# A Mamba block with attention and FFN on one core: six products on GpSimd instead of four, and their rows of C loaded in the last unit

## The chip, the cores and the metric

The kernel runs on one core of a Trainium2 chip. The metric is the device time of one execution in microseconds, from the first to the last instruction of the program with what lies around it; the lower, the better.

## What is computed

The input x is (8, 96, 64, 64): 8 batches, 96 channels, 4096 positions. Layer 0 is a group norm, a Mamba block (selective scan) and a residual. Layer 1 is linear attention and an FFN with rounding to an 8-bit float, each with a layer norm and a residual. The change concerns the selective scan alone, which runs over L = 4096 positions for 192 inner channels and 16 states:

```
dA  = exp(delta[..., None] * A)
dBu = delta[..., None] * Bm[:, :, None, :] * u[..., None]
h   = dA_t * h + dBu_t                     # for each position t
y_t = einsum('ben,bn->be', h, C_t)         # sum over the 16 states
y   = y + u * D
y   = y * silu(z);  out = y @ out_proj_w.T;  layernorm(out)
```

## The kernel before

The eight batches are taken as four pairs p. A pair's 4096 positions are cut into 8 chunks c of T = 512, so there are 32 chunks. The state of a scan is carried from chunk to chunk.

In a chunk the scan has 24 **units** u. `where(u)` (L555) gives j = u // 8 (three blocks of 64 inner channels), g = (u // 2) % 4 (four groups of four states) and b = u % 2 (half of the channels); a unit is 128 partitions (4 states x 32 channels) by 2 batches by 512 positions. The work of one unit, in the order in which `unit` (L611) issues it:

- `pooled` (L667): if the unit before is in POOLED, its product pr = hs * C is issued here on GpSimd, with C from an SBUF tile `c`.
- `rows_c` (L566): for the next unit, unless that is in POOLED, a matmul on TensorE (L571) spreads the rows of C over the partitions into a PSUM tile `cc` (two buffers).
- `sums` (L588): on even units, matmuls on TensorE (L595) add the products of two units, over their states, into the PSUM tile `y`. For pooled units the call stands elsewhere (L656 before the change).
- waiting norm work on GpSimd, then part 0 of the unit's steps.
- `products_b` (L558): dbu = du * B on GpSimd, three units ahead (AHEAD = 3, four buffers).
- the scans (L639): two instructions on VectorE, which need the decay `da` in PSUM (two buffers); behind each, `decay` (L575) issues the exponential of the next unit on ScalarE (L581).
- in each eighth unit `gate` (L607) on VectorE multiplies y with silu(z), and `skip` (L600) opens the next y.
- part 1 of the steps, and last, unless the unit is pooled, the product pr = hs * cc on VectorE (L663).

`hs`, a scan's output, has three buffers; a pooled product (`pq`) has two, another product four.

All other work is cut into pieces, by generators, and a table STEPS, written by hand, says which pieces are issued in which unit and part. P is the projection of the chunk after the next (convolution L450, SiLU L483 and L484, x_proj L489, its copies L494 and L497, dt_proj L507, delta L511). E is the output of the chunk before (projection L691, its copy L699, gains L718, transposes L707 with the additions L741 and L746, Gram products L759). F0 and F1 are the attention and FFN of an older chunk, from chunk 9 on (transposes L831, copy L834, L838, transposes L854, rounding L857, first layer L864 with L871, second layer L903, copy L908, end L915). G is the group norm of the next pair.

SILU = 10 is a unit after which ScalarE loads another table and runs the SiLU; the decays of unit 12 are issued ahead of it, into two other PSUM banks.

Before the change POOLED is (2, 3, 10, 11) and POOLED_G = 1: the units of group 1 for j = 0 and j = 1. The tile `c` has one buffer. `rows` (L541) fills it for the next chunk by four DMAs of 128 KB, issued by SP in unit 17, where group 1 of j = 0 and 1 has been used. [...]

Of the kernel before, what the change touches and what calls it, by code (L numbers as in the profile page):

```python
# [19 lines left out]
NU = NJ * NG * 2  # L20
# [1 line left out]
NK = T // 128  # L22
HID = 384
RANK = 6
POOLED = (2, 3, 10, 11)
POOLED_G = 1
SILU = 10
ROWS_B = (16, 18, 20, 22)
AHEAD = 3
# [36 lines left out]
def tile_mamba_linear_attention_ffn(  # L66
# [62 lines left out]
    def rsqrt(out_, var, eps):  # L129

        nc.gpsimd.tensor_scalar_add(out_, var, eps)
        nc.gpsimd.tensor_tensor(  # L132
            out_, out_, mhalf[0 : out_.shape[0], 0 : out_.shape[1]], op=ALU.pow
        )
# [245 lines left out]
    def later(kind, work):  # L380
        if kind in waiting:
            waiting[kind].append(work)
        else:
            work()

    def now(kind):
        for work in waiting[kind]:
            work()
        waiting[kind].clear()

    def norm_stats(src, n, tag):

        mv = p2.tile([128, n, 2], F32, tag=f"mv{tag}", name="mv")
        rstd = p2.tile([128, n], F32, tag=f"rs{tag}", name="rs")
        nmr = p2.tile([128, n], F32, tag=f"nm{tag}", name="nm")
        st = p2.tile([128, n, 6], F32, tag=f"st{tag}", name="st")
        for i in range(n):
            nc.vector.bn_stats(st[:, i, :], src[:, i, :])  # L398
        for i in range(n):
            nc.vector.bn_aggr(mv[:, i, :], st[:, i, :])  # L400

        def ends():
            nc.gpsimd.tensor_scalar_mul(nmr, mv[:, :, 0], -1.0)  # L403
            rsqrt(rstd, mv[:, :, 1], 1e-5)
            nc.gpsimd.tensor_mul(nmr, nmr, rstd)

        later("norms", ends)
        return rstd, nmr
# [132 lines left out]
    def rows(s, to, of, g):  # L541

        t = s[to, g] = p2.tile([128, 2, T], F32, tag=to, name=to, bufs=NG if to == "b" else 1)
        for n in range(NG):
            nc.sync.dma_start(
                t[32 * n : 32 * n + 32],
                s["bd"][of : of + 2 * NS].rearrange("(b n) t -> n b t", b=2)[NG * g + n]
                .unsqueeze(0)
                .to_broadcast([32, 2, T]),
            )  # L550

    def rows_b(s, g):
        rows(s, "b", 0, g)

    def where(u):  # L555
        return u // (2 * NG), (u // 2) % NG, u % 2

    def products_b(s, u):  # L558
        j, g, b = where(u)
        dbu = s["dbu", u] = p2.tile([128, 2, T], F32, tag="dbu", name="dbu", bufs=AHEAD + 1)  # L560
        nc.gpsimd.tensor_mul(  # L561
            dbu, s["du", j][:, 2 * b : 2 * b + 2, :],
            s["b", g][:, b, :].unsqueeze(1).to_broadcast([128, 2, T]),
        )

    def rows_c(s, u):  # L566
        j, g, b = where(u)
        if u in POOLED:
            return
        cc = s["cc", u] = ps_all.tile([128, T], F32, tag="cc", name="cc", bufs=2)  # L570
        nc.tensor.matmul(  # L571
            cc, lhsT=sel[64:128, g, b], rhs=s["cs"][64:128, :], start=True, stop=True
        )

    def decay(s, u, h, bank=None):  # L575
        if ("da", u, h) in s:
            return
        j, g, b = where(u)
        da = psum(bank) if bank else ps_all.tile([128, T], F32, tag="da", name="da", bufs=2)
        s["da", u, h] = da  # L580
        nc.scalar.activation(  # L581
            da, s["dl", j][:, 2 * b + h, :], AF.Exp, scale=aneg[:, 2 * j + h, g : g + 1]
        )
# [4 lines left out]
    def sums(s, u):  # L588

        j, g, _ = where(u)  # L590
        for b in range(2):
            pr = s.pop(("pr", u - 1 + b))
            for h in range(2):
                q = 64 * b + 32 * h
                nc.tensor.matmul(  # L595
                    s["y"][q : q + 32, :], lhsT=ssum, rhs=pr[:, h, :],
                    start=False, stop=(g == NG - 1),
                )

    def skip(s, j):  # L600

        s["y"] = ps_all.tile([128, T], F32, tag="y", name="y", bufs=1)
        nc.tensor.matmul(  # L603
            s["y"], lhsT=dd[:, j, :], rhs=s["xm"][:, j, :], start=True, stop=False
        )

    def gate(s, j):  # L607
        zs = s["zs"][:, j, :]
        nc.vector.tensor_mul(zs, s["y"], zs)  # L609

    def unit(s, prev, nxt, first, u, steps):  # L611
        def at(v):
            return (s, v) if v < NU else (nxt, v - NU)


        if u - 1 in POOLED:
            pooled(s, u - 1)
        if u:
            nc.scalar.copy(state["new"][:, u - 1, :], s.pop(("hs", u - 1))[:, :, T - 1])  # L619
        else:  # L620
            if prev is not None:
                nc.scalar.copy(state["new"][:, NU - 1, :], prev.pop(("hs", NU - 1))[:, :, T - 1])
            state["last"] = state.get("new")
            state["new"] = p2.tile([128, NU, 2], F32, tag="state", name="state")
        to, v = at(u + 1)
        if to is not None:
            rows_c(to, v)
        if u % 2 == 0 and (u or prev is not None) and (u - 1) not in POOLED:
            sums(s if u else prev, (u or NU) - 1)
        now("norms")  # L630
        steps(u, 0)
        to, v = at(u + AHEAD)
        if to is not None:
            products_b(to, v)
        hs = s["hs", u] = p2.tile([128, 2, T], F32, tag="hs", name="hs", bufs=3)
        dbu = s.pop(("dbu", u))
        to, v = at(u + 1)
        for h in range(2):
            nc.vector.tensor_tensor_scan(  # L639
                hs[:, h, :], s.pop(("da", u, h)), dbu[:, h, :],  # L640
                0.0 if first else state["last"][:, u, h : h + 1], ALU.mult, ALU.add,
            )
            if to is not None:
                decay(to, v, h)
        now("others")

        new = u % (2 * NG) == 1
        if new and u > 1:
            gate(s, u // (2 * NG) - 1)
        elif new and prev is not None:  # L650
            gate(prev, NJ - 1)
        if u == SILU and (nxt is not None):
            for h in range(2):
                decay(s, u + 2, h, ("mp", "mE")[h])
        steps(u, 1)
        if u - 4 in POOLED and u % 2:  # L656
            sums(s, u - 4)
        if new:
            skip(s, u // (2 * NG))
        if u in POOLED:  # L660
            return
        pr = s["pr", u] = p2.tile([128, 2, T], F32, tag="pr", name="pr", bufs=4)
        nc.vector.tensor_mul(  # L663
            pr, hs, s.pop(("cc", u)).unsqueeze(1).to_broadcast([128, 2, T])
        )

    def pooled(s, u):  # L667
        j, g, b = where(u)
        pr = s["pr", u] = p2.tile([128, 2, T], F32, tag="pq", name="pr")
        nc.gpsimd.tensor_mul(  # L670
            pr, s["hs", u], s["c", g][:, b, :].unsqueeze(1).to_broadcast([128, 2, T])
        )
# [5 lines left out]
    def chain_e(p, c, s):  # L678
# [51 lines left out]
        projected(1, ps)  # L730
        yield
        norm = norm_stats(o, 2 * NK, "o")
        yield
        for part in range(4):
# [197 lines left out]
    for g in range(NG):  # L932
        rows_b(slots[0], g)
    rows(slots[0], "c", 2 * NS, POOLED_G)
    spread(slots[0], 0)
# [46 lines left out]
    with tc.manual_schedule():  # L982
        for u in range(AHEAD):
            products_b(slots[0], u)
        for h in range(2):
            decay(slots[0], 0, h)
        rows_c(slots[0], 0)
        for i, (p, c) in enumerate(chunks):
            s = slots[i]
            prev = slots[i - 1] if i else None  # L990
            nxt = slots[i + 1] if i + 1 < N else None

            def steps(u, part):
                if part == 0:
                    if u in (0, 2 * NG):
                        spread(s, 1 + u // (2 * NG))
                    if nxt is not None and u == 18:
                        spread(nxt, 0)
                    if nxt is not None and u in ROWS_B:
                        rows_b(nxt, ROWS_B.index(u))  # L1000
                    if nxt is not None and u == 17:
                        rows(nxt, "c", 2 * NS, POOLED_G)
                for name in (STEPS[u] + "|").split("|")[part].split():
                    step(name, i, u)

            for u in range(NU):
                unit(s, prev, nxt, c == 0, u, steps)
# [4 lines left out]
    s = slots[N - 1]  # L1012
# [69 lines left out]
```

## Time and profile before

| | |
|---|---|
| median of 3 runs | 3535.59 us (3532.91 to 3539.99) |
| profiled execution | 3550.77 us, span 3549.1 us |
| TensorE (PE) busy | 2708.4 us, 76% |
| VectorE (DVE) busy | 3017.3 us, 85% |
| ScalarE (ACT) busy | 2277.4 us, 64% |
| GpSimd (POOL) busy | 2689.0 us, 76% |
| mean granted TensorE clock | 0.730 |
| DMA, mean | 125 GB/s |

Busy shares are means over all stages. A line of the groups gives line, engine, operation, output <- inputs, shapes and count, then busy us and the mean ns of one, then the idle time of the engine just before these instructions and what ended it. A line of the waits reads: engine and line that waited <- what ended the wait: us in total, times, longest us. A line of the timeline gives start, length, engine, line, operation and tiles, and in brackets the idle time before it. A matmul in 32-bit floats stands as two instructions in the counts.

### The profile page before, as it was taken

To read this page: it belongs to the slowest core of one execution; us is meant where nothing else is said; L and a number is where in the kernel's file an instruction comes from. 1 tells how busy PE (TensorE), PEld (TensorE's weight loads), DVE (VectorE), ACT (ScalarE), POOL (GpSimd) and SP (SyncE) were. 2 spreads that over 40 slices of the span, in tenths; PEclk is the share of its full clock that TensorE was granted. 3 is DMA by queue.
4 is the path that set the end of the run, shared out by engine and by line. 5 is a ranking of instruction groups with operands and counts; after the bars stand their busy time and mean duration, and the time that the engine had idled before them with its cause. 6 is when DMAs were issued, how large, how long until landed. Compare 5 with 4: busy or idle time off the path is not lost.

```text
span 3549.1 us, 35756 instructions
## 1 busy us (share of the span) xinstructions
PE 2708.4 (76%) x9770; PEld 1011.7 (29%) x9770; DVE 3017.3 (85%) x4345; ACT 2277.4 (64%) x4347; POOL 2689.0 (76%) x1838
## 2 busy tenths in 40 slices
PE   5577777778787777877878877777788787887677
PEld 1122222222223222322223322222233232332244
DVE  2699999899998889888889888899888888988934
ACT  2456666566666666666666666666776766676556
POOL 1778888788878787778777778778877878777734
PEclk8667777677766787776787677778866777775667
DMA  2555555555554456554456554455544445545212
GB/s 80 127 128 139 134 141 142 143 131 133 136 149 107 104 139 154 138 129 108 112 139 154 131 138 105 117 134 150 149 124 121 99 121 144 152 119 139 72 59 61
DMA packets 252399, 444.05 MB, mean 125 GB/s; under 512 B 36965, under 2 KB 53542, under 8 KB 252198
## 3 DMA queue, kind: packets, MB, share of 16 engines
q1 hardware_dynamic: 248982, 441.70, 49.2%
q8 instruction: 77, 1.26, 0.2%
q14 instruction: 124, 1.02, 0.1%
q10 hardware_dynamic: 3216, 0.07, 0.1%
HBM read 349.24 MB, written 92.41 MB: 124 GB/s over the span
## 4 chain that ended last, share of the span: by engine, by line
DVE 39%; PE 25%; ACT 12%; issue 9%; POOL 7%; DMA 2%; SPq 1%; DVEq 0%; POOLq 0%; ACTq 0%
DVE hs L639 25%; PE mp L450 7%; DVE pr L663 7%; PE y L595 4%; POOL dbu L561 3%; DVE st L398 3%; ACT da L581 2%; PE cc L571 2%; PE mE L759 2%; PE mp L507 1%; PE mp L489 1%; PE mE L691 1%; POOL pr L670 1%; DVE mv L400 1%; DMA b<-bd 1%
## 5 line engine op out<-in xcount | busy, mean ns | idle before, releaser
L561 POOL TENSOR_TENSOR dbu<-du,b 128x1024 f32<-128x1024 f32 x768 | 1802.9, 2362 | 220.2 <-DVE hs L639 106.7
L639 DVE TENSOR_TENSOR_SCAN hs<-da,state,dbu 128x512 f32<-128x512 f32 x1290 | 1575.7, 1267 | 260.3 <-ACT da L581 252.2
L581 ACT ACTIVATE da<-dl,aneg 128x512 f32<-128x512 f32 x1474 | 999.1, 688 | 780.9 <-DVE hs L639 777.8
L663 DVE TENSOR_TENSOR pr<-hs,cc 128x1024 f32<-128x1024 f32 x640 | 777.6, 1215 | 36.8 <-DVE hs L639 0.5
L595 PE MATMUL y<-pr,ssum 128*32 128x512 f32 x3072 | 633.9, 883 | 4.9 <-DVE pr L663 4.9
L571 PE MATMUL cc<-cs,sel 64*128 64x512 f32 x640 | 397.2, 623 | 292.1 <-DVE pr L663 291.6
L450 PE MATMUL mp<-u,wk 96*64 96x512 f32 x1536 | 428.1, 683 | 90.3 <-ACT xm L468 86.9
L571 PEld LDWEIGHTS cc<-cs,sel 64*128 64x128 f32 x640 | 145.4, 229 | 932.3 <-DVE pr L663 423.0
L670 POOL TENSOR_TENSOR pr<-hs,c 128x1024 f32<-128x1024 f32 x128 | 301.7, 2357 | 122.6 <-DVE hs L639 96.4
L639 DVE TENSOR_TENSOR_SCAN hs<-da,dbu 128x512 f32<-128x512 f32 x184 | 213.5, 1207 | 110.9 <-ACT da L581 110.6
L884 POOL CAST h<-h 128x512 fp8e5<-128x512 f16 x192 | 117.5, 614 | 155.9 <-ACT h L881 109.9
L603 PE MATMUL y<-xm,dd 128*128 128x512 f32 x192 | 157.2, 913 | 99.5 <-DVE zs L609 99.3
L403 POOL TENSOR_SCALAR nm<-mv 128x8 f32<-128x8 f32 (+1 forms) x128 | 32.6, 255 | 238.8 <-DVE mv L400 222.0
L489 PE MATMUL mp<-xm,xpT 128*96 128x512 f32 x192 | 158.7, 994 | 48.7 <-ACT xm L483 48.0
L507 PE MATMUL mp<-dbl,dtT 12*128 12x512 f32 x192 | 168.0, 968 | 34.6 <-ACT cs L497 33.3
L864 PE MATMUL mF<-qT,w1T 96*128 96x512 fp8e5 x153 | 67.9, 444 | 157.1 <-ACT h L871 156.4
L450 PEld LDWEIGHTS mp<-u,wk 96*64 96x64 f32 x1536 | 105.0, 151 | 286.3 <-issue 162.9
L132 POOL TENSOR_TENSOR rs<-rs,mhalf 128x8 f32<-128x8 f32 (+1 forms) x128 | 173.5, 1355 | 10.7
L595 PEld LDWEIGHTS y<-pr,ssum 128*32 128x32 f32 x3072 | 75.2, 128 | 271.9 <-issue 228.1
L691 PE MATMUL mE<-woT,zs 128*128 128x192 f32 x768 | 142.9, 336 | 5.9 <-ACT t1e L699 4.3
L458 PE MATMUL mp<-u,wz 96*64 96x512 f32 x384 | 134.8, 788 | 14.6 <-ACT xm L476 11.7
L619 ACT COPY state<-hs 128x2 f32<-128x2 f32 x736 | 131.5, 179 | 0.2
(214 smaller groups left out, 3468.1 us busy)
## 6 DMA issues: line engine op xcount, KB each, us to landing
du<-lu SPq DMA_DIRECT2D x384, 256.0 KB, 5.2
dl<-ld SPq DMA_DIRECT2D x384, 256.0 KB, 7.2
b<-bd SPq DMA_DIRECT2D x512, 128.0 KB, 6.0
ld<-delta SPq DMA_DIRECT2D x96, 256.0 KB, 4.4
lu<-du SPq DMA_DIRECT2D x96, 256.0 KB, 4.9
c<-bd SPq DMA_DIRECT2D x128, 128.0 KB, 3.2
t1d<-t1e SPq DMA_DIRECT2D x32, 388.0 KB, 4.7
tp<-t1d SPq DMA_DIRECT2D x64, 194.0 KB, 5.9
```

The costliest lines, as they stand in the source:

```text
L132: nc.gpsimd.tensor_tensor(out_, out_, mhalf[0 : out_.shape[0], 0 : out_.shape[1]], op=ALU.pow)
L450: nc.tensor.matmul(ps[64 * b : 64 * b + 64, :], lhsT=wk[:, k, 64 * j : 64 * j + 64], rhs=u[:, b, k : k + T], start=(k == 0), stop=(k == 3),)
L489: nc.tensor.matmul(ps[0:C, :], lhsT=xpT[:, j, :], rhs=xm[:, j, :], start=(j == 0), stop=(j == NJ - 1),)
L507: nc.tensor.matmul(ps, lhsT=dtT[:, j, :], rhs=dbl[0 : 2 * RANK, :], start=True, stop=True)
L561: nc.gpsimd.tensor_mul(dbu, s["du", j][:, 2 * b : 2 * b + 2, :], s["b", g][:, b, :].unsqueeze(1).to_broadcast([128, 2, T]),)
L571: nc.tensor.matmul(cc, lhsT=sel[64:128, g, b], rhs=s["cs"][64:128, :], start=True, stop=True)
L581: nc.scalar.activation(da, s["dl", j][:, 2 * b + h, :], AF.Exp, scale=aneg[:, 2 * j + h, g : g + 1])
L595: nc.tensor.matmul(s["y"][q : q + 32, :], lhsT=ssum, rhs=pr[:, h, :], start=False, stop=(g == NG - 1),)
L639: nc.vector.tensor_tensor_scan(hs[:, h, :], s.pop(("da", u, h)), dbu[:, h, :], 0.0 if first else state["last"][:, u, h : h + 1], ALU.mult, ...
L663: nc.vector.tensor_mul(pr, hs, s.pop(("cc", u)).unsqueeze(1).to_broadcast([128, 2, T]))
L670: nc.gpsimd.tensor_mul(pr, s["hs", u], s["c", g][:, b, :].unsqueeze(1).to_broadcast([128, 2, T]))
L691: nc.tensor.matmul(ps[:, 2 * k * C : 2 * (k + 1) * C], lhsT=zs[:, j, tok : tok + 128], rhs=woT[:, j].rearrange("p b c -> p (b c)"), start= ...
```

## The change

POOLED becomes (4, 5, 12, 13, 20, 21), the units of group 2 for all three j, and POOLED_G becomes 2. The sums of a pooled pair are called at the start of an even unit, three after the pair's second unit, instead of at the end of an odd unit, four after it. The next chunk's rows of C are loaded in the last unit, 23, instead of in unit 17.

```diff
-POOLED = (2, 3, 10, 11)
-POOLED_G = 1
+POOLED = (4, 5, 12, 13, 20, 21)
+POOLED_G = 2
...
         to, v = at(u + 1)
         if to is not None:
             rows_c(to, v)
+        if u - 3 in POOLED and u % 2 == 0:
+            sums(s, u - 3)
         if u % 2 == 0 and (u or prev is not None) and (u - 1) not in POOLED:
             sums(s if u else prev, (u or NU) - 1)
         now("norms")
...
         steps(u, 1)
-        if u - 4 in POOLED and u % 2:
-            sums(s, u - 4)
         if new:
             skip(s, u // (2 * NG))
...
                         rows_b(nxt, ROWS_B.index(u))
-                    if nxt is not None and u == 17:
+                    if nxt is not None and u == NU - 1:
                         rows(nxt, "c", 2 * NS, POOLED_G)
```

## The prediction

> **What bounds the kernel now.** I read the page's busy shares, then its groups by line, then the waits of VectorE alone, then the timeline of one ordinary chunk.
>
> ```profile
> PE 2708.4 (76%) x9770; PEld 1011.7 (29%) x9770; DVE 3017.3 (85%) x4345; ACT 2277.4 (64%) x4347; POOL 2689.0 (76%) x1838
> ...
> L561 POOL TENSOR_TENSOR dbu<-du,b 128x1024 f32<-128x1024 f32 x768 | 1802.9, 2362 | 220.2 <-DVE hs L639 106.7
> ...
> L663 DVE TENSOR_TENSOR pr<-hs,cc 128x1024 f32<-128x1024 f32 x640 | 777.6, 1215 | 36.8 <-DVE hs L639 0.5
> ...
> L670 POOL TENSOR_TENSOR pr<-hs,c 128x1024 f32<-128x1024 f32 x128 | 301.7, 2357 | 122.6 <-DVE hs L639 96.4
> ```
>
> VectorE is the busiest engine, but no engine is full. A unit costs it two scans of about 1.25 us and, unless pooled, a product of 1.215 us. Where it idles, one releaser dominates. The waits of VectorE from 1160 us to the last chunk:
>
> ```profile
> DVE hs L639 <- ACT da L581: 233.2, 85, 6.4
> ```
>
> So VectorE loses time only where the decay da is late. By scan starts there are two regimes: chunks 1 to 8, without the late FFN chain F, take 94.4 us with 88.5 us of VectorE work; chunks 9 to 30 take 105.4 with 92.5. The idle time of the second kind lies, per chunk, in unit 4 (1.8 us), 12 (6.0), 15 (2.9) and 21 (0.8); of the first kind almost only in unit 12 (3.9). The timeline of chunk 14 (start us, length, engine, line, tiles, idle before and its releaser) shows who is late:
>
> ```profile
> 1529.03 1.49 ACT L483 ACTIVATE xm<-xm 128x1536 f32<-128x1536 f32 x1
> 1532.51 0.58 PE L864 MATMUL mF<-qT,w1T 96*128 96x512 fp8e5 x1 [7.57 <-ACT h L871]
> 1533.02 0.79 PE L571 MATMUL cc<-cs,sel 64*128 64x512 f32 x1
> 1537.81 2.46 DVE L639 TENSOR_TENSOR_SCAN hs<-da,state,dbu 128x512 f32<-128x512 f32 x2 [6.01 <-ACT da L581]
> 1538.68 0.58 ACT L494 COPY dbl<-mp 96x512 f32<-96x512 f32 x1 [0.25 <-PE mp L489]
> ...
> 1543.28 1.94 PE L595 MATMUL y<-pr,ssum 128*32 128x512 f32 x8
> 1549.55 0.59 ACT L834 COPY tT<-mE 97x512 f32<-97x512 f32 x1 [4.75 <-PE mE L831]
> 1552.63 2.46 DVE L639 TENSOR_TENSOR_SCAN hs<-da,state,dbu 128x512 f32<-128x512 f32 x2 [3.40 <-ACT da L581]
> ...
> 1572.07 0.79 PE L571 MATMUL cc<-cs,sel 64*128 64x512 f32 x1 [2.90 <-DVE pr L663]
> 1578.45 0.59 ACT L857 ACTIVATE qT<-mF 96x512 fp8e5<-96x512 f32 x1 [2.70 <-PE mF L854]
> ```
>
> Unit 12 waits for ScalarE's own block of SiLU and table loads. Units 15 and 21 wait for ScalarE, which waits for TensorE (L831, L854), which has worked without a gap. So the second half of a chunk is bound by TensorE and ScalarE in turn; GpSimd bounds nothing.
>
> **What the Trainium skill says.** *PSUM — Partial Sum Buffer*, "Engine vs sequencer instructions": ScalarE, VectorE and GpSimd take instructions strictly in order, and matmuls start and complete in program order. The trace agrees: the cc of unit 13 (0.79 us) stands behind an L864 that waited 7.57 us. *GPSIMD Engine Reference*, "3.1 Elementwise": about 2.6 cycles an element at 1.2 GHz for two inputs; as an estimate 1024 x 2.6 / 1.2 = 2.2 us; the trace has 2.36, which I use. *SBUF — State Buffer*, "Who interferes with whom": a VectorE instruction with at most one SBUF input doesn't contend with GpSimd. Scan and product have one input in PSUM, and scans wholly beside GpSimd work averaged 1261 ns against 1258 ns without. *TensorE: Matmul & The Clock Gate*, "What's actually happening": TensorE falls to half clock after an idle window and rises after a busy one. Eight sums took 1.94 us at 1543 us and 1.07 at 569 us.
>
> **The change, part by part**, per chunk, against the profiled execution (3550.77 us, of which span 3549.1; the median 3535.59 is 0.9957 of it).
>
> *VectorE:* four products come back (units 2, 3, 10, 11: +4.86 us), six go (4, 5, 12, 13, 20, 21: -7.29), net -2.43 us. *TensorE:* two cc fewer (2 x 0.62). The sums move: units 2 and 3 from the end of unit 7 to the start of 4, 10 and 11 from the end of 15 to 12, 12 and 13 from 14 to 16. The sums of 20 and 21 are never issued: the new call needs an even unit three after 21, which is 24, and no chunk has one. So y lacks group 2 of the third j, and eight L595 instructions (1.07 to 1.94 us) vanish in each chunk. *GpSimd:* +2 x 2.36 = +4.7 us. *SP:* the four c loads move from unit 17 to 23, where they wait for the product of unit 21.
>
> First pair (2, 3 to 4, 5). VectorE has the same work before unit 6. The idle 1.8 us of unit 4 counts from the last scan of unit 3 and shifts with it. But the sums of 2 and 3 (1.07 to 1.94) now stand ahead of the second L691 group, less one cc (0.5); ScalarE's L699, ahead of the decays of unit 6, waits for L691. In chunk 4 that group ran from 495.4 to 497.6 us. Scan 3 ended at 494.1; products 2 and 3 put the end of product 3 at 496.6; with 1.24 us of sums and 2.2 of L691, L699 starts at 500.1 instead of 497.7. L699, L476 and one decay (starts 0.4 and 0.6 apart, 0.7 long) let scan 6 start at 501.8; it started at 501.4: a loss of 0.4. In chunks with F the pooled units gain about as much as L691 loses: 0.
>
> Second pair (10, 11 to 12, 13). Products 10 and 11 fall into the wait of unit 12 and cost nothing (if that wait were gone, 2.43 us); leaving out product 12 gains nothing for the same reason. The sums of 10 and 11 now stand ahead of L489, in place of one cc: 1.94 - 0.79 = 1.15 us later. L494 had 0.25 us of wait for L489 already, so the decays of unit 14 come about 1.1 later, and the 1.2 us of product 13 is eaten by that. Then 1.94 us of sums leave the row L489, L507, L595, L903, L831 that ends the wait of unit 15: 1.94 - 1.15 = -0.8 us. Without F there is no wait in unit 15, and I take -0.1.
>
> Third pair (20, 21). -2.43 us on VectorE, but with F the decays of unit 22 wait for L857, it for L854, and that chain starts at product 19 and loses only its cc (0.79): -0.8 us, the rest becomes idle time before unit 22. Without F the next limit is L468 (idle 1.18 us behind L450) ahead of the decay of unit 23: in chunk 4 it started at 569.1 and the decay was done at 570.3; a cc less (0.79) makes that 569.5, so scan 23 starts at 569.6 instead of 571.2: -1.6.
>
> GpSimd: 83.4 us busy of 105.4 becomes 88.1 of about 104. It idles 5.4 us in units 22, 23 and 0, which takes the 4.7 of the third pair; dbu runs three units ahead; 4.7 us of idle time in unit 16 cover the second pair. Price 0; without that cover 4.7. The c loads: 4 x 0.43 us of issue, data needed in unit 5, some 20 us later: 0; without cover, up to 1.7 for what stands behind them on SP. The pooled products hold hs, of three buffers, for longer. From the end of scan 20 in chunk 14 GpSimd has 1.2 us of the dbu of unit 23, product 20, the next dbu and product 21 to do (3 x 2.36), so the hs of unit 21 is free 8.3 us later; the scan that needs it, of the next unit 0, starts about 11 us later: 0, and 1 to 2 if GpSimd were late. The dropped sums lie beside VectorE's work: 0 to -0.5, taken as 0.
>
> Sum: without F -0.4 + 0.1 + 1.6 = 1.3 us gained, x 9 chunks = 12; with F 0 + 0.8 + 0.8 = 1.6, x 23 = 37. In all 49 us: 3550.8 - 49 = 3501.8; x 0.9957 = 3487 on the median's scale.
>
> **Rivals.**
>
> *VectorE bounds throughout* (0.20). 2.43 x 32 = 78 us: 3458. For it: 85% busy, idle 4 us a chunk early. Against: units 12, 15 and 21.
>
> *The sums moved forward hold up ScalarE* (0.22), the slower side. The place is TensorE's order: L691 and L489 behind sums. At half clock the first costs 0.9 us, the second 0.9 if the wait of unit 15 then doesn't shrink, because a TensorE idle for longer runs at half clock. 1.8 x 32 = 58, less the third pair's 9 x 1.6 + 23 x 0.8 = 33: 25 us slower, 3560. It decides once the two delays exceed 1.0 us a chunk.
>
> *GpSimd takes it back* (0.08). If dbu or the FFN's casts fall behind in the last units, 4.7 us more on GpSimd against 2.43 off VectorE: no change, 3536. For it: few idle stretches; against: the lead of three units.
>
> That the change drops sums is no rival but certain from the code; issued, they would cost up to 0.5 us a chunk, 16 in all.
>
> **How the numbers follow.** My forecast has 0.50, alone 3465 to 3515 (half and one and a half times the gain, roughly). 3445 is the second case with 0.4 us a chunk of shorter waits; 3552 takes in two thirds of the slower rival's loss. Faster by over 0.2% (7 us, about what a measurement of this kernel tells from no change): 0.50 + 0.20 = 0.70; same 0.08; slower 0.22.
>
> **What would show it.** L663 x576 (32 x 18), L670 x192, cc x576, L595 x2816 instead of 3072; VectorE busy 78 us less; its wait in unit 12 shorter by 1.2 us, in unit 15 by about 0.8, and a new wait of 1 to 2 us ahead of unit 22. L489 should start a microsecond later after the SiLU. I am wrong if scans wait for dbu, if GpSimd's idle time ahead of L561 vanishes, or if unit 15 waits as long as now.

## The result and the profile after

The changed kernel took 3501.97 us in the median of four runs (3488.33 to 3507.47), beside 3537.79 us for the kernel before, measured with it. The ratio is 0.9894, with a 95% interval from 0.986 to 0.9928: faster by about 36 us. The forecast was 3487 us. The profiled execution, the slowest of the four, took 3507.47 us, of which span 3505.7; before, the span was 3549.1. So the span fell by 43.4 us where the sum of the forecast had 49. As the forecast says, the changed kernel leaves out the sums of units 20 and 21, so its y lacks group 2 of the third block; e1 below issues them.

From L403 on, a line of the changed kernel carries a number that is one to three higher than before: the product L663 is now L664, the pooled product L670 is L671, the scan L639 is L642, the decay L581 is L582, the sums L595 are L596, and L489 and L494 are L490 and L495.

First the page: the busy shares, and then four groups of instructions (line, engine, operation, tiles, count | busy us, mean ns of one | idle time before them and its releaser).

```profile
PE 2688.1 (77%) x9450; PEld 1013.9 (29%) x9450; DVE 2948.9 (84%) x4281; ACT 2272.5 (65%) x4347; POOL 2833.9 (81%) x1902
...
L562 POOL TENSOR_TENSOR dbu<-du,b 128x1024 f32<-128x1024 f32 x768 | 1803.3, 2363 | 168.5 <-DVE hs L642 138.4
...
L596 PE MATMUL y<-pr,ssum 128*32 128x512 f32 x2816 | 656.2, 908 | 132.7 <-DVE pr L664 132.6
L664 DVE TENSOR_TENSOR pr<-hs,cc 128x1024 f32<-128x1024 f32 x576 | 698.4, 1212 | 33.5 <-DVE hs L642 0.9
...
L671 POOL TENSOR_TENSOR pr<-hs,c 128x1024 f32<-128x1024 f32 x192 | 453.1, 2360 | 50.9 <-DVE hs L642 50.1
```

The counts are those that the forecast gave: 576 products on VectorE, 192 on GpSimd, 2816 sums. The product group lost 777.6 - 698.4 = 79.2 us, as forecast (78). VectorE's busy time lost only 68.4: it counts the time in which two records overlap once, and in the new order they overlap less, 290.0 us in all instead of 304.7. GpSimd took on 145 us, and its idle time ahead of the dbu products shrank from 220.2 to 168.5 us without being used up. TensorE is the odd row: it does 320 instructions fewer, yet its busy time fell by only 20 us.

Then the waits of VectorE from chunk 11 up to the last chunk (who waited <- who ended it: us, times, longest).

```profile
DVE hs L642 <- ACT da L582: 220.5, 93, 4.9
DVE hs L642 <- POOL h L885: 11.0, 6, 3.3
DVE hs L642 <- POOL dbu L562: 9.7, 4, 3.0
...
DVE hs L642 <- POOL pr L671: 2.5, 1, 2.5
```

The decay still ends nearly all of it (233.2 us before). Scans wait longer for GpSimd than before, but only some 23 us in 20 chunks (4.9 before).

Last the timeline of chunk 14, the one shown before (start us, length, engine, line, operation and tiles, and in brackets the idle time before it).

```profile
1522.62 1.48 ACT L484 ACTIVATE xm<-xm 128x1536 f32<-128x1536 f32 x1
...
1526.09 0.58 PE L865 MATMUL mF<-qT,w1T 96*128 96x512 fp8e5 x1 [7.49 <-ACT h L872]
...
1526.61 1.94 PE L596 MATMUL y<-pr,ssum 128*32 128x512 f32 x8
...
1528.47 4.55 PE L490 MATMUL mp<-xm,xpT 128*96 128x512 f32 x6
...
1531.39 2.46 DVE L642 TENSOR_TENSOR_SCAN hs<-da,state,dbu 128x512 f32<-128x512 f32 x2 [4.64 <-ACT da L582]
...
1533.07 0.58 ACT L495 COPY dbl<-mp 96x512 f32<-96x512 f32 x1 [1.05 <-PE mp L490]
...
1542.39 0.59 ACT L835 COPY tT<-mE 97x512 f32<-97x512 f32 x1 [3.42 <-PE mE L832]
...
1545.47 2.46 DVE L642 TENSOR_TENSOR_SCAN hs<-da,state,dbu 128x512 f32<-128x512 f32 x2 [2.06 <-ACT da L582]
...
1571.46 0.59 ACT L858 ACTIVATE qT<-mF 96x512 fp8e5<-96x512 f32 x1 [3.21 <-PE mF L855]
...
1572.73 1.28 DVE L642 TENSOR_TENSOR_SCAN hs<-da,state,dbu 128x512 f32<-128x512 f32 x1 [2.83 <-ACT da L582]
```

Behind the same L865, which still waits 7.5 us, the eight sums of products 10 and 11 now stand ahead of L490, and the copy L495 waits 1.05 us for it instead of 0.25. The wait of unit 12 is 4.64 us (6.01 before), that of unit 15 is 2.06 (3.40), and a new one of 2.83 us stands ahead of unit 22, behind L858. These are the steps that the forecast named. Whether they had the forecast sizes is read from means over chunks: A are chunks 1 to 8, without the FFN, and B chunks 10 to 30, with it. The table gives the change of a mean chunk against before in us, worked out from the starts of the scans in the profiled executions, of which there is one for each kernel; a minus is a gain. The last two columns belong to two experiments below.

| stretch of a chunk | forecast | changed kernel | e1 | e5 |
|---|---|---|---|---|
| A, units 0 to 9 | +0.4 | +2.0 | +0.75 | +0.75 |
| A, units 10 to 17 | -0.1 | -0.65 | -0.6 | -0.6 |
| A, units 18 to 23 | -1.6 | -2.3 | -2.2 | -2.4 |
| **A, chunk of 94.4** | **-1.3** | **-1.0** | **-2.0** | **-2.2** |
| B, units 0 to 9 | 0 | +0.25 | -0.4 | +0.4 |
| B, units 10 to 17 | -0.8 | -2.1 | -1.9 | -2.2 |
| B, units 18 to 23 | -0.8 | +0.3 | -0.5 | -0.15 |
| **B, chunk of 105.7** | **-1.6** | **-1.5** | **-2.8** | **-2.0** |

The totals agree with the forecast, and the terms do not. The question for the experiments was therefore which terms are real.

### The profile page after: what moved, and what is told of

The parts are those of the page before. It is cut to its first block, busy times and chain, and to the rows that moved or that the text cites. A ratio compares the mean times of both kernels' runs of the same rounds, so it can differ in the third digit from the quotient of the medians.

```text
span 3505.7 us, 35136 instructions
## 1 busy us (share of the span) xinstructions
PE 2688.1 (77%) x9450; PEld 1013.9 (29%) x9450; DVE 2948.9 (84%) x4281; ACT 2272.5 (65%) x4347; POOL 2833.9 (81%) x1902
## 4 chain that ended last, share of the span: by engine, by line
DVE 39%; PE 24%; ACT 11%; issue 9%; POOL 8%; DMA 5%; SPq 0%; DVEq 0%; POOLq 0%; ACTq 0%
DVE hs L642 25%; DVE pr L664 6%; PE mp L451 6%; PE y L596 4%; POOL dbu L562 3%; DVE st L398 3%; PE mp L490 3%; ACT da L582 2%; PE mE L692 2%; DMA dl<-ld 1%; PE mE L760 1%; PE cc L572 1%; DVE mv L400 1%; PE mp L508 1%; POOL rs L132 1%
## 5 line engine op out<-in xcount | busy, mean ns | idle before, releaser
L562 POOL TENSOR_TENSOR dbu<-du,b 128x1024 f32<-128x1024 f32 x768 | 1803.3, 2363 | 168.5 <-DVE hs L642 138.4
L642 DVE TENSOR_TENSOR_SCAN hs<-da,state,dbu 128x512 f32<-128x512 f32 x1290 | 1578.1, 1267 | 279.5 <-ACT da L582 248.7
L582 ACT ACTIVATE da<-dl,aneg 128x512 f32<-128x512 f32 x1474 | 996.0, 688 | 733.0 <-DVE hs L642 730.4
L596 PE MATMUL y<-pr,ssum 128*32 128x512 f32 x2816 | 656.2, 908 | 132.7 <-DVE pr L664 132.6
L664 DVE TENSOR_TENSOR pr<-hs,cc 128x1024 f32<-128x1024 f32 x576 | 698.4, 1212 | 33.5 <-DVE hs L642 0.9
L572 PE MATMUL cc<-cs,sel 64*128 64x512 f32 x576 | 348.9, 607 | 276.9 <-DVE pr L664 276.6
L671 POOL TENSOR_TENSOR pr<-hs,c 128x1024 f32<-128x1024 f32 x192 | 453.1, 2360 | 50.9 <-DVE hs L642 50.1
L451 PE MATMUL mp<-u,wk 96*64 96x512 f32 x1536 | 449.3, 713 | 20.8 <-ACT xm L469 17.0
L572 PEld LDWEIGHTS cc<-cs,sel 64*128 64x128 f32 x576 | 127.4, 222 | 681.1 <-DVE pr L664 393.3
L642 DVE TENSOR_TENSOR_SCAN hs<-da,dbu 128x512 f32<-128x512 f32 x184 | 213.7, 1206 | 116.9 <-ACT da L582 116.2
L596 PEld LDWEIGHTS y<-pr,ssum 128*32 128x32 f32 x2816 | 87.6, 136 | 610.1 <-issue 308.3
L865 PE MATMUL mF<-qT,w1T 96*128 96x512 fp8e5 x153 | 72.9, 476 | 159.3 <-ACT h L872 158.4
L604 PE MATMUL y<-xm,dd 128*128 128x512 f32 x192 | 144.6, 844 | 44.6 <-DVE zs L610 44.3
L508 PE MATMUL mp<-dbl,dtT 12*128 12x512 f32 x192 | 150.6, 874 | 31.2 <-ACT cs L498 27.6
L451 PEld LDWEIGHTS mp<-u,wk 96*64 96x64 f32 x1536 | 108.5, 156 | 218.1 <-issue 176.6
L692 PE MATMUL mE<-woT,zs 128*128 128x192 f32 x768 | 149.7, 347 | 10.1 <-DVE x L845 6.8
L692 PEld LDWEIGHTS mE<-woT,zs 128*128 128x128 f32 x768 | 130.7, 199 | 75.1 <-DVE x L845 18.7
L490 PE MATMUL mp<-xm,xpT 128*96 128x512 f32 x192 | 134.1, 854 | 0.9 <-ACT zs L482 0.7
```

The lines of the kernel that those rows point to most:

```text
L451: nc.tensor.matmul(ps[64 * b : 64 * b + 64, :], lhsT=wk[:, k, 64 * j : 64 * j + 64], rhs=u[:, b, k : k + T], start=(k == 0), stop=(k == 3),)
L490: nc.tensor.matmul(ps[0:C, :], lhsT=xpT[:, j, :], rhs=xm[:, j, :], start=(j == 0), stop=(j == NJ - 1),)
L508: nc.tensor.matmul(ps, lhsT=dtT[:, j, :], rhs=dbl[0 : 2 * RANK, :], start=True, stop=True)
L562: nc.gpsimd.tensor_mul(dbu, s["du", j][:, 2 * b : 2 * b + 2, :], s["b", g][:, b, :].unsqueeze(1).to_broadcast([128, 2, T]),)
L572: nc.tensor.matmul(cc, lhsT=sel[64:128, g, b], rhs=s["cs"][64:128, :], start=True, stop=True)
L582: nc.scalar.activation(da, s["dl", j][:, 2 * b + h, :], AF.Exp, scale=aneg[:, 2 * j + h, g : g + 1])
```

## The experiments

**The theory at the outset**, for e1 to e4, was the forecast's: the second half of a chunk is paced by TensorE and ScalarE in turn, the new place of the sums moves that pace, and the dropped sums hardly matter. Its rival was that the gain is the dropped work itself. e1 contradicted both, and a second theory took their place. **The clock**: without the eight sums TensorE is less busy around the turn of the chunk, so it runs at half clock in the units behind it, and the matmuls that ScalarE waits for come late. Its rival: the sums act in another way, and matmuls without an effect on any value change nothing.

All edits are to the changed kernel, except in e9. Of the kernels below, e2, e4, e5 and e7 leave out the same sums as the changed kernel; the others issue the sums of every unit. All ratios are to the kernel before, measured with each, and have their 95% intervals.

### e1: the missing sums, issued in unit 0 of the next chunk

```diff
+        if u == 0 and prev is not None and NU - 3 in POOLED:
+            sums(prev, NU - 3)
...
+    if NU - 3 in POOLED:
+        sums(s, NU - 3)
```

> The changed kernel with the sums of units 20 and 21 issued again, in unit 0 of the next chunk. Theory (dropped sums lie beside VectorE's work): TensorE is busy 3.1 of 4.3 us in unit 0, so the eight matmuls of 1.1 to 1.9 us cost 0 to 0.5 us a chunk, 0 to 16 us: ratio to the kernel before 0.989 to 0.994. Rival (the gain is nothing but work left out, TensorE bounds units 20 to 0): the full 1.1 to 1.9 us in 32 chunks, 35 to 60 us: ratio 0.999 to 1.006.

Measured: 3466.56 us, 0.9807 (0.9776 to 0.9837). Both expectations missed, on the other side: issuing the sums makes the kernel 0.87% faster, some 31 us, and its interval lies wholly below that of the changed kernel. By stretches the gain is 1.2 us in units 0 to 9 of A, 0.6 there in B and 0.75 in the last units of B (for which see the slow chunks at e6). The theory of the clock comes from this run; e5 tests it.

### e2: the sums of products 2, 3 and 10, 11 at the end of units 4 and 12

```diff
-        if u % 2 == 0 and (u or prev is not None) and (u - 1) not in POOLED:
+        late = u in (4, 12)
+        if u % 2 == 0 and (u or prev is not None) and (u - 1) not in POOLED and not late:
             sums(s if u else prev, (u or NU) - 1)
...
         steps(u, 1)
+        if late:
+            sums(s, u - 1)
```

> The changed kernel with the sums of units 2, 3 and of 10, 11 issued at the end of units 4 and 12, behind the steps, instead of at their start ahead of L692 and L490. Theory (these sums hold up ScalarE's copies L700 and L495 and so the decays): the wait of unit 5 in chunks without F goes (1.4 us x 9), that of unit 13 shrinks (0.7 x 9 and 1.4 x 22): 13 + 20 to 35 us less, ratio 0.979 to 0.984. Rival (TensorE's row is full, the sums only delay the next matmul instead): ratio 0.987 to 0.992.

Measured: 0.9863 (0.984 to 0.9886), between the two expectations, with overlap with the changed kernel's interval. Units 10 to 17 of B gain 1.45 us more, as the place of the sums ahead of L490 would have it; the units 0 to 9 lose 1.2 of it again, 0.8 of that in unit 0, and the last units gain 1.0.

### e3, e4, e7: one pair less on GpSimd

```diff
-POOLED = (4, 5, 12, 13, 20, 21)
+POOLED = (4, 5, 12, 13)          # e3
+POOLED = (12, 13, 20, 21)        # e4
+POOLED = (4, 5, 20, 21)          # e7
```

> The changed kernel with units 20 and 21 multiplied on VectorE again (POOLED = 4, 5, 12, 13), their sums issued. Theory (with F the third pair gains nothing, its 2.43 us turn into a wait for L855 and a TensorE that stays at half clock): 2.3 us a chunk lost without F (x 9 = 21), -0.5 to +0.3 with F (x 23): 10 to 28 us above the changed kernel, ratio 0.992 to 0.997. Rival (VectorE bounds throughout): 2.43 x 32 = 78 us, ratio 1.011.

> The changed kernel with units 4 and 5 multiplied on VectorE as well (POOLED = 12, 13, 20, 21), so no unit of the first block is pooled. Theory (part of the pair's 2.43 us is eaten by the waits of units 4 and 5): 1.0 us a chunk lost without F, 1.2 to 1.5 with F: 35 to 45 us above the changed kernel, ratio 0.999 to 1.002. Rival (VectorE bounds there): 78 us, ratio 1.011.

> The changed kernel with units 12 and 13 multiplied on VectorE again (POOLED = 4, 5, 20, 21); the sums of units 10, 11 and 12, 13 stand in units 12 and 14. Theory (the second pair gains with F because its sums leave the row that ends the wait of unit 15; product 12 lies in the wait of unit 12): with F 1.0 to 2.0 us a chunk lost, without F 0.5 to 1.2: 28 to 57 us above the changed kernel, ratio 0.997 to 1.005. Rival (VectorE bounds): 78 us, 1.011; the other rival (the pair's gain came only from freeing units 10 and 11, whose products lie in the SiLU wait anyway): 0 to 10 us, ratio 0.989 to 0.992.

Measured: e3 3502.82 us, 0.991 (0.9887 to 0.9934); e4 3563.73 us, 1.0079 (1.0052 to 1.0106); e7 3506.52 us, 0.991 (0.9882 to 0.9937). The theory missed each time: e3 lies just below its range, e4 between it and the rival, and e7 in the range of its second rival.

In e3 units 20 and 21 are multiplied on VectorE and their sums are issued as before. Its ratio is that of the changed kernel within the intervals: the third pair with its sums dropped is worth nothing that can be measured. Beside e1, which pools the pair and issues its sums, the pair is worth 0.991 - 0.9807 = 0.0103, about 36 us. In e4 the loss beside the changed kernel is some 65 us. By stages a chunk of B loses 2.3 us of the 2.66 us that two more products take (a unit with a product lasts 1.33 us longer than one without, in the starts of the scans), a chunk of A only 0.8: the first units of B are VectorE's own. In e7 nothing is lost beyond the intervals. Units 10 to 17 do lose 0.65 to 0.73 us a chunk, but the units 0 to 9 of A gain 0.8 and the last units of B gain 1.0. So the second pair gains in its place what is lost elsewhere; for B, three chunks of the changed kernel explain most of it (shown at e6). By the totals alone, the second rival of e7 isn't excluded.

### e5: idle matmuls in the place of the missing sums

The matmul that spreads the rows of C for unit 1, issued in unit 0, is repeated four times into the same bank; the values are the same, and the sums stay missing.

```diff
-        nc.tensor.matmul(
-            cc, lhsT=sel[64:128, g, b], rhs=s["cs"][64:128, :], start=True, stop=True
-        )
+        for _ in range(4 if u in (1,) else 1):
+            nc.tensor.matmul(
+                cc, lhsT=sel[64:128, g, b], rhs=s["cs"][64:128, :], start=True, stop=True
+            )
```

> The changed kernel (the sums of 20 and 21 still missing) with the cc matmul of unit 1, issued in unit 0, repeated: four times the same write instead of once, so three matmuls of 0.5 to 0.8 us more for TensorE in each chunk, that change no value. Theory (the sums brought back in unit 0 helped because TensorE, kept busy, runs at full clock in units 1 to 5): clock in units 1 to 4 from 0.62-0.85 to over 0.9, the waits of units 4 and 5 shorter by 0.7 to 0.9 us a chunk: ratio to before 0.980 to 0.985. Rival (the sums helped by what they do or where they stand, not by activity): three matmuls more are only work, ratio 0.989 to 0.996.

Measured: 3485.73 us, 0.9848 (0.9813 to 0.9883), as expected; its interval overlaps with that of the changed kernel, so the stretches have to carry the reading. In A the mean granted clock of units 1 to 3 goes from 0.70 to 0.96 (0.96 in e1 as well), and the gain in units 0 to 9 is the same 1.2 us as with the sums (table). Chunk 7 shows it matmul by matmul. The timeline of the changed kernel, from unit 1 to scan 6:

```profile
767.52 3.68 PE L451 MATMUL mp<-u,wk 96*64 96x512 f32 x8
...
773.86 1.94 PE L596 MATMUL y<-pr,ssum 128*32 128x512 f32 x8
775.73 3.15 PE L692 MATMUL mE<-woT,zs 128*128 128x192 f32 x12
...
781.67 2.22 PE L692 MATMUL mE<-woT,zs 128*128 128x192 f32 x12
...
785.74 2.46 DVE L642 TENSOR_TENSOR_SCAN hs<-da,state,dbu 128x512 f32<-128x512 f32 x2 [2.53 <-ACT da L582]
```

The same stretch in e5 (a line further down from L573 on):

```profile
752.25 1.16 PE L573 MATMUL cc<-cs,sel 64*128 64x512 f32 x4 [0.34 <-DVE pr L665]
...
756.27 1.94 PE L451 MATMUL mp<-u,wk 96*64 96x512 f32 x8
...
760.36 1.07 PE L597 MATMUL y<-pr,ssum 128*32 128x512 f32 x8
761.36 2.22 PE L693 MATMUL mE<-woT,zs 128*128 128x192 f32 x12
...
768.30 2.22 PE L693 MATMUL mE<-woT,zs 128*128 128x192 f32 x12
...
772.36 2.46 DVE L643 TENSOR_TENSOR_SCAN hs<-da,state,dbu 128x512 f32<-128x512 f32 x2 [0.38 <-ACT da L583]
```

The clock over units 1 to 3 of this chunk, first in the changed kernel, then in e5 (stretch: its length, then busy us and instructions of PE, PEld, DVE, ACT and POOL, then the mean granted clock, the DMA share and GB/s):

```profile
766.93:778.40 11.47, 11.33 (x31) 4.61 (x32) 11.26 (x11) 4.68 (x10) 8.57 (x5) 0.55 0.90 251
```

```profile
755.71:767.18 11.47, 9.98 (x44) 3.86 (x44) 11.26 (x11) 5.05 (x11) 9.19 (x5) 1.00 1.02 257
```

The eight L451 matmuls take 3.68 us in the one and 1.94 in the other, the eight sums 1.94 and 1.07, and the first L692 group 3.15 and 2.22. The second L692 group, which L700 and with it the decay of unit 6 wait for, starts 14.2 us after this L451 group in the changed kernel and 12.0 after it in e5; VectorE waits 2.53 us ahead of scan 6 in the one and 0.38 in the other. Idle matmuls with no effect on any value cure this wait, so what the changed kernel loses to e1 in these units of A is the clock and not what the sums compute. In B the clock of units 1 to 3 was not raised by e5 (0.85 in both), and units 0 to 9 gained nothing (table); in e1 it was raised there too, to 0.98, and they gained 0.6.

The single chunks of B show it best. Eleven of the kernels pool units 4 and 5. In their chunks of B, without 14 and 22, unit 4 lasted 3.31 or 3.32 us in each of the 148 chunks in which the mean clock of units 1 to 3 was above 0.85, and 3.96 to 7.00 us in each of the 61 in which it was 0.73 or less. (In chunks 14 and 22 it lasted 4.8 to 4.9 us at any clock from 0.75 to 1.) The whole stretch need not follow: in e6, e8, e11 and e12 the clock there was 0.93 to 0.97, yet units 0 to 9 of B lasted 0.65 to 1.75 us longer than before, because unit 0 had grown to between 5.2 and 6.2 us (4.4 in the changed kernel; see e12).

The place of the sums counts, too. e3 issues the sums of units 20 and 21, but in unit 22, and its clock in units 1 to 3 of A was 0.72, where the kernel before had 0.90; its units 0 to 9 of A lasted 1.2 us longer than before. So of the 1.2 us that e1 gains there beside the changed kernel, about 0.5 seem to come from matmuls standing in unit 0; e3 differs from e1 in the third pair as well, so this is not shown.

### e6 and e11: sums back, and idle matmuls in units 19 and 11 as well

Unit 20 is pooled and needs no rows of C, so its free bank takes four idle matmuls (e6); e11 adds seven for unit 12, issued in unit 11. Both have the sums of e1.

```diff
+WARM = {20: 4}                   # e11: {12: 7, 20: 4}
...
         if u in POOLED:
+            if u in WARM:
+                cc = ps_all.tile([128, T], F32, tag="cc", name="cc", bufs=2)
+                for _ in range(WARM[u]):
+                    nc.tensor.matmul(
+                        cc, lhsT=sel[64:128, g, b], rhs=s["cs"][64:128, :], start=True, stop=True
+                    )
             return
```

> The kernel with the sums brought back, and four idle cc matmuls in unit 19, where TensorE waits for the product of unit 19 (into the cc bank that pooled unit 20 doesn't need). Theory (the wait ahead of unit 22, 2.8 us with F, is L451 at half clock): units 20 and 21 run near full clock, L451's eight matmuls take 1.9 instead of 2.7 us and the sums of unit 20 1.1 instead of 1.9, scan 22 starts 0.8 to 1.5 us earlier in 23 chunks, 0.3 to 0.8 in the others: 20 to 40 us under the kernel with the sums back, ratio 0.970 to 0.976. Rival (the clock isn't released by so little, or the idle matmuls delay the sums): ratio 0.980 to 0.985.

> The kernel of 0.9744 with seven more idle cc matmuls in unit 11, where TensorE stands still during the SiLU (into the bank that pooled unit 12 doesn't need). Theory (the sums of 10 and 11 and L490 ahead of L495 run at half clock, 1.9 and 4.9 us): at full clock 1.1 and 2.6, so the wait of unit 13 (0.8 and 1.3 us) goes and L832 comes earlier, the wait of unit 15 (0.75) too: 1.0 to 2.0 us a chunk, 30 to 60 us: ratio 0.957 to 0.966. Rival (idle matmuls delay what follows, or the clock falls again behind L865's wait): 0.972 to 0.980.

Measured: e6 3448.56 us, 0.9744 (0.9722 to 0.9766), as expected and apart from e1's interval. In the mean of B, unit 21 with the wait ahead of unit 22 lasted 5.64 us in the changed kernel, 5.40 in e1 and 4.17 in e6. Chunk 10 of the changed kernel, where the wait was long, shows what e6 removes (timeline of TensorE and VectorE from unit 20 to the next unit 1):

```profile
1136.65 3.68 PE L451 MATMUL mp<-u,wk 96*64 96x512 f32 x8
1140.26 1.09 PE L855 MATMUL mF<-ident,o 128*96 128x128 f32 x4
...
1142.66 2.46 DVE L642 TENSOR_TENSOR_SCAN hs<-da,state,dbu 128x512 f32<-128x512 f32 x2 [4.42 <-ACT da L582]
...
1153.30 3.68 PE L451 MATMUL mp<-u,wk 96*64 96x512 f32 x8
...
1160.50 2.46 DVE L642 TENSOR_TENSOR_SCAN hs<-da,state,dbu 128x512 f32<-128x512 f32 x2 [3.27 <-POOL h L885]
```

And e6 in the same chunk, where the idle matmuls are L573:

```profile
1107.64 2.07 PE L573 MATMUL cc<-cs,sel 64*128 64x512 f32 x4 [1.04 <-DVE pr L673]
1109.64 3.61 PE L603 MATMUL y<-pr,ssum 128*32 128x512 f32 x8
1113.19 0.95 PE L769 MATMUL mE<-t1e 128*97 128x97 f32 x8
1114.06 1.94 PE L452 MATMUL mp<-u,wk 96*64 96x512 f32 x8
...
1117.88 1.28 DVE L651 TENSOR_TENSOR_SCAN hs<-da,state,dbu 128x512 f32<-128x512 f32 x1 [1.56 <-ACT da L589]
```

From 1107.64 us on TensorE's records show no gap, the next L452 group takes 1.94 us instead of 3.68, and the wait ahead of unit 22 is 1.56 us instead of 4.42. Chunk 10 of the changed kernel is one of three (10, 13 and 16) whose TensorE ran at or near half clock from unit 20 into the next chunk (mean clock 0.50, 0.62 and 0.50); in these the stretch from scan 18 to the next scan 1 lasted 32 to 35 us, in the other chunks of B 26 to 28. About half of the 41 us between the profiled executions of the changed kernel and e1 lies in these three chunks. In e1 and e7 no chunk did so, in e5 one did, and in e8, which issues the sums, two. So the missing sums are not needed for it, and what starts such a spell stays open.

e11 measured 3446.92 us, 0.9741 (0.9721 to 0.9761), not the large gain that the theory gave it. In A the clock of unit 12 rose from 0.56 to 0.68, and units 10 to 17 gained 0.7 us. In B it stayed at 0.55, and they gained nothing.

### e8 and e12: the sums of products 10 and 11 behind L490

e8 is e1, and e12 is e11, each with the delay of e2 in unit 12 alone.

```diff
+        late = u in (12,)
```

> The kernel with the sums of 20 and 21 brought back, and the sums of units 10 and 11 issued at the end of unit 12, behind L490, instead of at its start. Theory (they hold up L495 and the decays of unit 14, and with F the delay reaches unit 15): with F 1.0 to 1.5 us a chunk less, without F 0 to 0.5 more: 20 to 33 us under the kernel with the sums back, ratio 0.972 to 0.976. Rival (TensorE's order there doesn't matter): 0.979 to 0.983.

> As the kernel with idle matmuls in units 11 and 19, and the sums of units 10 and 11 behind L490, at the end of unit 12. Theory (at full clock these sums are 1.1 us ahead of L490, which still reach L495): 0 to 0.8 us a chunk less than with the sums ahead, ratio 0.953 to 0.966. Rival (behind L490 they delay L508 and what ends the wait of unit 15): 0.5 to 1.0 us a chunk more, 0.965 to 0.975.

Measured: e8 3461.57 us, 0.9773 (0.9752 to 0.9795), between the expectations and within reach of e1's interval. Units 10 to 17 of B gain 1.5 us, the next unit 0 gives back 0.9, and A loses 0.6 in units 10 to 17 and 0.5 elsewhere. e12 measured 3443.22 us, 0.9728 (0.9706 to 0.975): the lowest time of all, but in the range of the rival, and its interval overlaps with those of e6 and e11. The waits of VectorE in e12, from 1110 to 3200 us, say what is next:

```profile
DVE hs L652 <- ACT da L589: 164.0, 101, 4.9
DVE hs L652 <- POOL h L897: 52.5, 21, 4.3
```

The wait for the decay has come down, and one for the FFN's casts on GpSimd, ahead of the next unit 1, has grown from 11.0 us in the changed kernel's like stretch to 52.5. Unit 0 of B lasts 4.3 us in e1, 5.4 in e6 and 6.2 in e12: here part of the gain of the warm clock is lost again.

### e9 and e10: idle matmuls in unit 19 where unit 20 is not pooled

e9 is the kernel before and e10 is e3, each with the rows of C for unit 20 spread four times instead of once.

```diff
+        for _ in range(4 if u in (20,) else 1):
```

> Control: the kernel before with the cc matmul of unit 20, issued in unit 19, repeated four times (same value). Theory (TensorE at full clock shortens the row that ends the wait of unit 21, 0.8 us with F): 10 to 25 us less than before, ratio 0.993 to 0.997; so the idle matmuls alone don't make the 0.974 of the kernel that has them beside the six pooled products. Rival (all of that gain is TensorE's clock and none is the products'): ratio 0.975 to 0.985.

> The changed kernel with units 20 and 21 on VectorE again (POOLED = 4, 5, 12, 13), sums issued, and the same four matmuls in unit 19 as the kernel of 0.9744. Theory (the third pair's 2.43 us are eaten by a slow TensorE, and count once that is at full clock): 1.0 to 2.0 us a chunk slower than 0.9744, 32 to 64 us: ratio 0.983 to 0.992. Rival (the pair gains nothing with F whatever the clock): 0.974 to 0.980.

Measured: e9 3545.4 us, 1.0021 (1.0009 to 1.0032), a miss; e10 3503.87 us, 0.9902 (0.9883 to 0.9922), that of e3. Neither made the condition that it was to test: the mean clock of units 20 and 21 in B was 0.50 and 0.83 in both. TensorE's timeline in e9, chunk 10:

```profile
1137.86 2.07 PE L572 MATMUL cc<-cs,sel 64*128 64x512 f32 x4 [1.04 <-DVE pr L664]
1141.56 0.79 PE L572 MATMUL cc<-cs,sel 64*128 64x512 f32 x1 [1.62 <-DVE pr L664]
...
1145.69 3.15 PE L450 MATMUL mp<-u,wk 96*64 96x512 f32 x8
```

With unit 21 on VectorE its rows of C stand ahead of the sums and wait for a product, so a gap of 1.62 us follows the idle matmuls. The L450 group behind it took 3.15 us, where that of e6 took 1.94, and the kernel became 0.2% slower. What the kernel before would gain at full clock is left open.

## Why the prediction was right, and where its terms were not

**The sum was right through two errors that cancel.** That it came out is in part luck. From the ratios, times 3536 us:

| term | forecast, us | measured, us | from |
|---|---|---|---|
| first and second pair | 16 | 32 | before and e3 |
| third pair, its sums issued | 33 | 36 | e3 and e1 |
| the sums dropped | 0 | -31 | e1 and changed kernel |
| together | 49 | 37 | |

(Forecast: 23 x 0.8 - 9 x 0.3 = 16 and 9 x 1.6 + 23 x 0.8 = 33. Each measured term has an uncertainty of about 8 to 16 us, from the intervals of its ratios.)

*Dropped sums.* The step that failed, in sign, is "The dropped sums lie beside VectorE's work: 0 to -0.5, taken as 0", with the remark that issued sums would cost up to 16 us. They lie beside VectorE's work, but TensorE's speed doesn't: e1 is 31 us faster with them in unit 0, and e5 gets about half of that from matmuls that compute nothing new. (By the ratios these are 16 us with an uncertainty of some 17; that the clock is behind it rests on the stretches and chunks shown at e5. The size of the 31 us is open too, because of the three slow chunks shown at e6.) A page of the Trainium skill bears on it. *TensorE: Matmul & The Clock Gate*, "What's actually happening", has the array fall to half clock after an idle window of some 3.4 us and rise after a busy one; the clock records here hold 0.5 and 1.0 alone, nearly all in multiples of 3.41 us. The forecast used it for the slower rival, but not on the matmuls that the change itself takes away.

*First pair.* The mechanism was the forecast one: sums ahead of L691 (now L692), L699 and the decay of unit 6 late. The size of 0.4 us in A was measured as 2.0; with the clock restored (e1, e5) 0.75 remains, and 1.25 is the clock. The term was worked out in a chunk where the matmuls ahead of L691 ran at full clock (eight of L450 in 1.94 us); in chunk 7 of the changed kernel they took 3.68. The forecast also left out that the sums of units 4 and 5 move from unit 6 to unit 8; units 8 and 9 together lasted 8.86 us in A before and after, and 8.54 and 8.63 in B.

*Second pair.* L490 starts 1.14 us later in the mean of B, as forecast (1.15). But it ends only 0.34 later, since it ran for 4.14 us instead of 4.94, at a mean clock of 0.68 instead of 0.57: the sums ahead of it had warmed TensorE (with these sums behind it, in e2 and e8, it took 4.94 and 4.75). The sums of units 12 and 13 left the row behind it, so the end of L832 came 2.1 us earlier and the wait of unit 15 fell from 2.92 to 0.79; the forecast had 0.8. That the sums still stand in L490's way is shown by e2 and e8, which gain about 1.5 us in this stretch, and lose more than half of that again by the next units 0 to 9.

*Third pair.* In A the last units gained 2.3 us against 1.6, but 0.5 of that stands in e3 as well, without this pair; in B the -0.8 turned into +0.3 (-0.4 without the three slow chunks). The sums of product 19 did end 0.73 us earlier, but L854 (now L855) ended only 0.16 earlier, because L451 ran at half clock. The new wait ahead of unit 22 is there, 3.1 us a chunk in B where 0.8 stood before. With the sums issued the pair gave 36 us, near its 33; e1's last units gain 1.7 us on e3's in A and 0.7 in B, so here the mechanism was right as well.

*GpSimd at price 0.* Right for the changed kernel: scans waited for dbu for 10.4 us in the whole execution. The loads of c, moved to unit 23, never held up a pooled product: of its 50.9 us of idle time before L671, 50.1 were ended by VectorE's scan. Moving the loads alone was not tried.

**The rivals.** *VectorE throughout*: against it stand the waits for the decay, 220.5 us of them after chunk 11, and e4 and e7, in which two more products cost 65 us and about 5. *The sums hold up ScalarE*: right on the place and on half clock, and in A its delay of 0.9 us was even too low; it didn't decide, because in B the wait of unit 15 shrank by more than L490 was delayed. *GpSimd takes it back*: not here, but in the fastest kernel, e12, GpSimd ends the second longest waits of VectorE (52.5 us).

## What to carry to other kernels

Before matmuls are removed or moved, look at what keeps TensorE's row unbroken: here the speed of what stood behind them depended on it, though the busiest engine was another one. Price a change stretch by stretch and test each term by itself, since a total that agrees may hide a term of the wrong sign. And where a unit is free, a few idle matmuls at the right place may be worth trying: here they gained where no gap followed them (e6), and not where one did (e9).

## What the runs showed of the hardware that was not expected

Leaving out eight short matmuls of 1.1 to 1.9 us in all from each chunk made the kernel 31 us slower than issuing them in unit 0 (e1), and sums and four idle matmuls a chunk together took it from a ratio of 0.9894 to 0.9744, by 1.5% (e6). The page named above puts the penalty of the ramp at under 1% of a typical span, for a TensorE that warms up once; here the clock went up and down all the time, in 316 stretches of 0.5 and 1.0 in turn over the 3505.7 us of the changed kernel, so that figure can't be carried over. Warming is not a matter of count alone: four matmuls without a gap behind them raised the clock of units 20 and 21 of B from 0.50 and 0.78 to 0.60 and 0.97 (e1 to e6), the same four with a gap of 1.62 us behind them did not raise it (e9), and seven in unit 11 raised that of unit 12 in A, from 0.56 to 0.68, but not in B (e11). How full a window must be is left open by these runs.
